# Two-layer graph attention on one core: the last step's order with v last, and the first step's norm and products in another order

## The chip, the cores and the metric

The kernel runs on one core of a Trainium2 chip. The metric is the device time of one execution in microseconds (us). Before the change the median of three runs is 3420.51 us (3420.47 to 3423.61). The core's engines are TensorE (PE in the profile; its weight loads are PEld), VectorE (DVE), ScalarE (ACT), GpSimd (POOL) and SyncE (SP), which issues nearly all DMAs. Each engine carries out its own queue in order.

## The reference

`x` holds 64 graphs of 256 nodes with 512 features, `adj` a 256x256 mask for each graph. Two layers follow each other, each with a residual:

```python
h = jnp.maximum(_layernorm(x, axis=-1), 0.0)
x = x + L0(h, adj)      # q, k, v = h@Wq, h@Wk, h@Wv   4 heads of 64; softmax(where(adj, q k^T / 8, -max)) v; @Wo + bo
h = jnp.maximum(_layernorm(x, axis=-1), 0.0)
x = x + L1(h, adj)      # layernorm(h)*gamma+beta, then w_qkv; 8 heads of 64; mask adj | eye; softmax; @w_out.T + b_out
```

All of it is float32. A row of `adj` without a neighbour gives an even average in layer 0; in layer 1 the diagonal is always allowed.

## The kernel before

`fast_path` takes the 64 graphs in 32 steps of two graphs (`G = 2`, `NSTEP = 32`). The 512 nodes of a step are four tiles of 128 rows (`NT`). Layer 1 of a step runs beside layer 0 of the next ones. A second function, `general_path`, is run only if a flag made from `extremes` says that a softmax sum was out of bounds; here it isn't run.

Steps are numbered from 0 to 31. A call such as `scores` (31, 1, 3) is step 31, layer 1, head pair 3; layer 1 has four pairs (0 to 3), layer 0 two. For each step:

- `load_h`, `load_x` bring in `x` twice, for the norm (`h`) and for the residual (`xt`). `norm0` takes the statistics of a tile on DVE (`moments`, L566 and L567), an inverse root is raised on POOL (`row_scales`, L574), and ACT scales the rows (L582; L598 in step 0).
- `transpose_h` (L641; `first_transposes`, L658, in step 0) turns `h` on TensorE; ACT evacuates it into `hT`.
- A product of two large matrices is computed as seven products of half-size blocks instead of eight (`PRODUCT` names the two blocks of each). Products 1 and 2 need raw blocks only; the others need sums of blocks: the weights' are made once (`weight_sum`, L405), those of `hT` and `oT1` in each step on POOL by `act_sums0` (block 3) and `act_sums1` (blocks 4, 5, 6), L408 to L413. `project_qk` (L741) and `project_v1` (L782) and `combine1` (L807) are such sets of seven; `project_v0` (L768) and `combine0` (L793) are plain. `evacuate` and `accumulate` add each product into its place on DVE or copy it on ACT. Some products share a PSUM bank (`SHARED`): product 2 goes on in the bank of product 1 once ACT has copied that.
- `scores` (L839) gives q k^T of a head pair into four PSUM banks, `mask_scores` adds the mask on DVE (L852), `exponentials` on ACT (L857) gives `p`, `key_halves` adds the two halves of the keys, on POOL (L865; on DVE for pairs 1 and 3 of step 31), for the sums.
- `weigh` multiplies `p` with v (L874), copies the result to `oT` on ACT (L888), and sums `pd` over the keys with a matrix of ones (L894). `invert` takes the reciprocals on DVE (L904), notes an extreme (L905), and copies them to the 64 partitions of each head with eight small DMAs (L916, into `invb`). `normalise` multiplies `oT` by `invb` (L921), on POOL, or on DVE for pairs 1 and 3 of the last step.
- `combine1` closes the step; `second_bias` (L621) has added the output's bias to `xt` on POOL beforehand, and `store` or, in step 31, `store_block` writes the result.

In steps 0 and 1 `neighbours` (L506), `neighbours_turn` (L524, L527) and `adjacency_turn` (L540) prepare the row `ne`, which tells whether a node has a neighbour, and the turned mask; `masks` makes `n0` and `n1`. `weight_block` (L463, L468) turns the four 512x512 blocks of w_qkv and w_out (block 3) on TensorE.

The order is written out by hand. A call `at(period, place, fn, ...)` puts a function at a place; the list is sorted by place, and the functions are called in that order. One unit of place is about one set of seven products, and a period is 6.13. TensorE, DVE, ACT and POOL take their instructions in this order:

```python
ctx.enter_context(tc.manual_schedule(engines={mybir.EngineType.PE, mybir.EngineType.DVE,
                                              mybir.EngineType.Activation, mybir.EngineType.Pool}))
```

SP is not in that list: the place of its transfers among each other comes from the framework's planner. `visit(period, w, prev, cur)` places one head pair's `weigh`, `invert` and `normalise` and another pair's `scores`, `mask_scores`, `exponentials` and `key_halves`. The PSUM banks of the products turn in a ring of four, `ps_sc` has four more for scores and weighings. Several SBUF buffers exist once: `inv`, `invb`, `pd`, `u`, `h`, `hT`.

## Time and profile before

| | us |
|---|---|
| runs, median of three | 3420.51 |
| profiled execution | 3424.45 |
| its span, first to last instruction | 3422.7 |
| TensorE busy in the span | 3383.6 |
| POOL busy | 1990.5 |
| DVE busy | 1907.1 |
| ACT busy | 1248.1 |
| one period in the middle, 210.57 to 315.26 (the first product set of layer 1, by the chain) | 104.69 |

The mean granted TensorE clock is 0.997. In a timeline row the first number is the start in us from the span's start, the second the length, then engine, line, operation, what is written and read; "x8" is the number of instructions merged in the row, and the bracket is the idle time of the engine before it and what ended that. In a row of the windows stand for each engine its busy us (and instructions) within the stretch, then the granted clock as a share of full speed, the busy share of the DMA engines and GB/s.

### The profile page before, as it was taken

The page shows a single profiled execution, that of the slowest core. Times are in us where ns is not written, and L with a number is a line of the kernel's source. Part 1 is how long each engine was busy: PE and PEld are TensorE (multiplying, and loading weights), DVE is VectorE, ACT ScalarE, POOL GpSimd, SP SyncE. Part 2 cuts the span into 40 slices and gives each one's busy share as a digit, 9 for nine tenths or more (in the row PEclk, how much of TensorE's full clock was granted, in tenths as well). Part 3 has the DMA queues.
Part 4 walks back from the last instruction along what each step waited for, and adds up shares of the span by engine and source line. Part 5 has one row for each costly group of instructions (what it writes and reads, how often), then busy time and mean ns, then how long its engine had stood idle before and what let it go on. Part 6 is the DMA issues. An engine that isn't in the chain of part 4 may idle for free.

```text
span 3422.7 us, 59225 instructions
## 1 busy us (share of the span) xinstructions
PE 3383.6 (99%) x22602; PEld 2627.8 (77%) x22602; DVE 1907.1 (56%) x3392; ACT 1248.1 (36%) x2201; POOL 1990.5 (58%) x1854
## 2 busy tenths in 40 slices
PE   8999999999999999999999999999999999999998
PEld 6787777777777877777777778777777777787766
DVE  5655556555565555565555655555655556555554
ACT  3433443333333333433333333334333433333421
POOL 5655665556655556655566555566555665555641
PEclk9999999999999999999999999999999999999999
DMA  3112111211111111111111112111111111211011
GB/s 128 42 58 56 38 50 46 57 57 54 32 47 56 58 56 34 53 47 56 57 54 32 47 57 58 57 30 52 52 56 56 55 32 46 57 58 50 22 42 38
DMA packets 167697, 173.89 MB, mean 51 GB/s; under 512 B 59624, under 2 KB 112368, under 8 KB 167408
## 3 DMA queue, kind: packets, MB, share of 16 engines
q1 hardware_dynamic: 167200, 169.91, 16.9%
q8 instruction: 180, 2.95, 0.4%
q14 instruction: 109, 0.89, 0.1%
q10 hardware_dynamic: 208, 0.14, 0.0%
HBM read 85.99 MB, written 33.62 MB: 35 GB/s over the span
## 4 chain that ended last, share of the span: by engine, by line
PE 97%; DVE 1%; ACT 0%; SPq 0%; DMA 0%; issue 0%; POOL 0%; ACTq 0%; DVEq 0%; POOLq 0%
PE mm L741 34%; PE mm L782 11%; PE mm L807 11%; PE sc L839 11%; PE sc L874 10%; PE mm L768 6%; PE mm L793 6%; PE mm L641 3%; PE mm L894 2%; PE mm L540 0%; SPq L916 0%; DVE inv L904 0%; ACT h L582 0%; DMA invb<-inv 0%; DVE bs L566 0%
## 5 line engine op out<-in xcount | busy, mean ns | idle before, releaser
L865 POOL TENSOR_TENSOR pd<-p 128x512 f32<-128x512 f32 x380 | 478.4, 1274 | 664.1 <-ACT p L857 564.0
L741 PE MATMUL mm<-hT,wqkv 128*128 128x256 f32 x3584 | 797.2, 381 | 0.0
L741 PEld LDWEIGHTS mm<-hT,wqkv 128*128 128x128 f32 x3584 | 673.3, 190 | 108.8 <-issue 21.1
L857 ACT ACTIVATE p<-p 128x512 f32<-128x512 f32 x768 | 459.2, 629 | 463.0 <-DVE p L852 462.0
L904 DVE RECIPROCAL inv<-mm 128x128 f32<-128x128 f32 x384 | 339.7, 926 | 374.4 <-PE mm L894 343.7
L852 DVE TENSOR_TENSOR p<-sc,n 128x512 f32<-128x512 f32 x768 | 481.1, 682 | 5.6 <-PE sc L839 5.6
L888 ACT COPY oT<-sc 128x512 f32<-128x512 f32 x192 | 112.3, 585 | 1007.9 <-PE sc L874 981.7
L741 PE MATMUL mm<-hT,wqk 128*128 128x256 f32 x1792 | 406.0, 384 | 2.5 <-DVE wqk L405 1.9
L807 PE MATMUL mm<-wo,oT 128*128 128x256 f32 x1792 | 396.1, 381 | 5.1 <-DVE oT L921 3.5
L921 POOL TENSOR_TENSOR oT<-oT,invb 128x512 f32<-128x512 f32 x190 | 241.9, 1273 | 270.7 <-DMA invb<-inv 244.5
L741 PEld LDWEIGHTS mm<-hT,wqk 128*128 128x128 f32 x1792 | 340.0, 191 | 72.3 <-DVE inv L904 9.9
L782 PE MATMUL mm<-wqkv,hT 128*128 128x256 f32 x1792 | 395.3, 381 | 0.0
L839 PE MATMUL sc<-qk 64*128 64x256 f32 x3072 | 384.2, 389 | 1.4 <-ACT oT L888 1.4
L874 PE MATMUL sc<-p,v 128*32 128x256 f32 x6144 | 377.6, 384 | 5.6 <-ACT p L857 5.6
L782 PEld LDWEIGHTS mm<-wqkv,hT 128*128 128x128 f32 x1792 | 337.8, 190 | 55.3 <-issue 10.6
L807 PEld LDWEIGHTS mm<-wo,oT 128*128 128x128 f32 x1792 | 339.8, 191 | 52.4 <-DVE oT L921 4.3
L839 PEld LDWEIGHTS sc<-qk 64*128 64x128 f32 x3072 | 281.2, 186 | 106.0 <-issue 77.8
L874 PEld LDWEIGHTS sc<-p,v 128*32 128x32 f32 x6144 | 181.3, 110 | 173.0 <-issue 64.6
L709 POOL TENSOR_TENSOR xt<-xt,u 128x512 f32<-128x512 f32 x93 | 118.0, 1269 | 246.4 <-DVE xt L702 183.9
L582 ACT ACTIVATE h<-h,mr,r 128x512 f32<-128x512 f32 x252 | 197.5, 809 | 118.9 <-POOL mr L578 118.8
L793 PE MATMUL mm<-wo,oT 128*128 128x512 f32 x512 | 230.3, 593 | 0.0
L768 PE MATMUL mm<-wv,hT 128*128 128x256 f32 x1024 | 230.2, 382 | 0.0
(112 smaller groups left out, 3664.0 us busy)
## 6 DMA issues: line engine op xcount, KB each, us to landing
invb<-inv SPq DMA_DIRECT2D x1532, 32.0 KB, 1.8
xt<-in_x_dram SPq DMA_DIRECT2D x32, 1024.0 KB, 5.5
h<-in_x_dram SPq DMA_DIRECT2D x31, 1024.0 KB, 5.4
out_dram<-xt SPq DMA_DIRECT2D x31, 1024.0 KB, 4.5
ne<-row SPq DMA_DIRECT2D x30, 256.0 KB, 4.1
ad<-in_adj_dram SPq DMA_DIRECT2D x32, 128.0 KB, 12.5
wr<-in_L_gnn_w_qkv_dram SPq DMA_DIRECT2D x3, 1024.0 KB
h<-in_x_dram SPq DMA_DIRECT2D x4, 256.0 KB, 3.8
```

The source lines that it names most:

```text
L741: nc.tensor.matmul(bank[:, k, :], w[:, wa, c, k, a * P:(a + 1) * P], st["hT"][:, ba, c, :], start=first and (k, c) == (0, 0), stop=(k, c) ...
L768: nc.tensor.matmul(bank, st["hT"][:, b0 + t // NIC * step, c % HC, i:i + P], wv0[:, c, :], start=(c == 0), stop=(c == NC - 1),)
L782: nc.tensor.matmul(bank[:, t, :], st["hT"][:, ba, c, t * P:(t + 1) * P], wqkv1[:, wa, c, 2, :], start=first and (t, c) == (0, 0), stop=(t, ...
L793: nc.tensor.matmul(bank, st["oT0"][:, pr, t // NIC, t % NIC * P:(t % NIC + 1) * P], wo0[:, pr, :], start=(pr == 0), stop=(pr == PR0 - 1),)
L807: nc.tensor.matmul(bank[:, t, :], st["oT1"][:, ba, c, t * P:(t + 1) * P], wo1[:, wa, c, :], start=first and (t, c) == (0, 0), stop=(t, c) ...
L839: nc.tensor.matmul(sc[g][e][:, kc, :], qk[rows, 1, k0:k0 + P], qk[rows, 0, g * N:(g + 1) * N], start=True, stop=True,)
L852: nc.vector.tensor_tensor(p[e][:, g], sc[e], neg[:, :, g, :], ALU.add)
L857: nc.scalar.activation(p[e][:, g], p[e][:, g], AF.Exp, scale=SCALE)
L865: engine_of(s, lyr, pr).tensor_tensor(pd[:, e], p[e][:, :, 0, :], p[e][:, :, 1, :], ALU.add)
L874: nc.tensor.matmul(po[r0:r0 + 32, g, :], st[f"v{lyr}"][:, g * NIC + kc, pr * P + r0:pr * P + r0 + 32], p[r0 // DH][:, g, kc, :], start=(kc ...
L904: nc.vector.reciprocal(inv[:, i * P:(i + 1) * P], sums[:, i * P:(i + 1) * P])
L921: engine_of(s, lyr, pr).tensor_tensor(dst, dst, invb, ALU.mult)
```

## The change

**The last step (31).**
- Layer 1's order was q and k of pairs 0 and 2, v, q and k of pairs 1 and 3, with each pair's weighing as soon as it was ready, and the combine at the end. It is now q and k (0, 2); step 30's combine; q and k (1, 3); v. The four pairs' scores, key sums and inverses lie between these products. The four weighings follow v directly, then the combine.
- `weigh` is split: `weigh_out` (as before, with the copy on ACT) and `key_sums`. In the last step `weigh_last` multiplies the PSUM result by `invb` on DVE as it writes `oT`, so ACT's copy and `normalise` are gone there.
- The transposes of step 31 come ahead of step 30's combine; its second statistics are taken close together, its scales two rows at a time; half of its `hT` is evacuated by DVE; `act_sums` of `hT` move to DVE. `second_bias` comes later.
- Step 30's pairs 1 and 3 are visited at other places, its combine comes later. Four pairs' `p`, `pd`, `inv` and `invb` live at once, so some use buffers of other tiles that are free by then (`h`, `oT0`, `v0`, `wo0`, `wv0`, `n0`, `ne`, `ab`, `u`). Half the copies of the inverses of pair 1 go out on ACT's queue, as those of pair 3 did already.

**The first steps.**
- `norm0` of step 0 is split: the statistics of the next tile go ahead of `first_scale` of the one before.
- Step 0's first set goes 1, 2, 6, 5, 7, 3, 4 instead of 1, 6, 5, 2, 7, 3, 4, with `adjacency_turn` before product 2.
- `neighbours_rows` (the four DVE instructions of L524) is taken out of `neighbours_turn` and placed earlier in step 1, ahead of step 0's first key sums.
- The four blocks of w_out are turned between the products of step 0's first set of layer 1, not before its scores. Step 0's `second_bias` comes later, its scales of layer 1 two rows at a time and earlier; odd chunks of its `hT` in layer 1 are evacuated by DVE.

The middle steps' calls stay as they are. The core of the diff:

```diff
+    def neighbours_rows(s):
+        rows = S[s]["rows"] = sm.tile([P, NT, P], BF, name="rows", tag="u", bufs=1)
+        for t in range(NT):
+            nc.vector.tensor_scalar(rows[:, t, :], onesb, S[s]["any"][:, t:t + 1], None, op0=ALU.mult)
...
+    def first_scale(t):
+        st = S[0]
+        r, mr = st["r"][:, t:t + 1], st["mr"][:, t:t + 1]
+        nc.vector.tensor_scalar(mr, st["mean"][:, t, 0:1], r, -1.0, op0=ALU.mult, op1=ALU.mult)
+        nc.scalar.activation(st["h"][:, t, :], st["h"][:, t, :], AF.Identity, bias=mr, scale=r)
...
+        part = 2 if s in (0, NSTEP - 1) else NT
+        if t % part == part - 1:
+            rows = slice(t + 1 - part, t + 1)
...
+            row_scales(s, ve, rows)
...
+        elif s in (0, NSTEP - 1) and c % 2:
+            nc.vector.tensor_scalar(
+                dst, ph, gb[:, 0, c:c + 1], gb[:, 1, c:c + 1], op0=ALU.mult, op1=ALU.add
+            )
...
+        last = (s, lyr) == (NSTEP - 1, 1)
+        if last and pr == 1:
+            both = act.tile([P, 2, G, NIC, N], FP, name="p", tag="h")
+            p = [both[:, e] for e in range(2)]
+        elif last and pr == 3:
+            p = [act.tile([P, G, NIC, N], FP, name="p", tag=tag) for tag in ("oT0", "v0")]
...
+    def weigh_last(pr):
+
+        po, dst = weigh(NSTEP - 1, 1, pr, pr == 0)
+        nc.vector.tensor_tensor(dst, po, S[NSTEP - 1]["invb", 1, pr], ALU.mult)
...
-                    queue = nc.scalar if d0 % DH and (s, lyr, pr) == (NSTEP - 1, 1, 3) else nc.sync
+                    queue = nc.scalar if d0 % DH and last and pr in (1, 3) else nc.sync
...
+    LAST_QK = 4.0
+    for s in range(-1, NSTEP - 1):
+        p, tail = s, s == NSTEP - 2
...
+        visit(p, 3.685 if tail else AT_Q0 + 2 / 7, (s, 1, 1, False), (s, 1, 3), 0.03 if tail else 0.0)
         if s >= 0:
-            visit(p, AT_V0, (s, 1, 3, False), (s + 2, 0, 0))
+            visit(p, LAST_QK + 3 / 7 if tail else AT_V0, (s, 1, 3, False), (s + 2, 0, 0))
+
+    none = (NSTEP,)
+    p = NSTEP - 2
+    for w, i, pr in (
+        (LAST_QK + 1, 5 / 7, 0), (LAST_QK + 1 + 3 / 7, 5 / 7, 2), (LAST_QK + 3, 5 / 7, 1), (LAST_QK + 3 + 2 / 7, 4 / 7, 3)
+    ):
+        visit(p, w, none, (NSTEP - 1, 1, pr))
+        at(p, w + i - 0.0005, key_sums, NSTEP - 1, 1, pr)
+        at(p, w + i, invert, NSTEP - 1, 1, pr)
+    for i, pr in enumerate((0, 1, 2, 3)):
+        at(p, LAST_QK + 4 + 0.01 * i, weigh_last, pr)
...
+            if s == 0:
+                at(p, 0.95 + 0.4 * t, first_scale, t)
...
-            at(p, (3.857, 3.59)[s], neighbours_turn, s)
+            at(p, (3.72, 2.72)[s], neighbours_rows, s)
+            at(p, (3.855, 3.59)[s], neighbours_turn, s)
...
+        order = SET if s else (1, 2, 6, 5, 7, 3, 4)
...
-            at(p, (3.55, 3.7, 4.05, 4.2)[t] - back, norm1_rest, s, t)
-            at(p, 3.62 + 0.08 * t, second_bias, s, t)
-            at(p, 4.5 + 0.1 * t - back, scale_row, s, t)
+            at(p, AT_C0 + 0.3 + 0.14 * t - back if (s, t) != (NSTEP - 1, 3) else 3.69, norm1, s, t)
+            at(p, ((3.55, 3.7, 4.05, 4.2) if s < NSTEP - 1 else (3.55, 3.6, 3.7, 3.705))[t] - back, norm1_rest, s, t)
+            at(p, 3.62 + 0.08 * t if 0 < s < NSTEP - 1 else 6.5 + 0.1 * t, second_bias, s, t)
+            at(p, 4.5 + 0.1 * t if 0 < s < NSTEP - 1 else (4.25 if s == 0 else 3.71) + 0.003 * t, scale_row, s, t)
...
+            at(p, (AT_H1 if s < NSTEP - 1 else 3.8) + 0.0001 * c, transpose_h, s, 1, c)
+        at(p, AT_C1 + 0.15 if s < NSTEP - 1 else 3.95, lambda s=s: act_sums0(S[s]["hT"], nc.gpsimd if s < NSTEP - 1 else nc.vector))
...
+            at_set(p, AT_C1 if not last else LAST_QK + 1, SETC, combine1, s)
...
+            at_set(p, LAST_QK, SET, project_qk, s, 1, 0)
+            at_set(p, LAST_QK + 2, SET, project_qk, s, 1, 1)
+            at_set(p, LAST_QK + 3, SET, project_v1, s)
+            at(p, LAST_QK + 4.015, lambda s=s: act_sums0(S[s]["oT1"], nc.vector))
+            at(p, LAST_QK + 4.035, lambda s=s: act_sums1(S[s]["oT1"], nc.vector))
+            at_set(p, LAST_QK + 4.1, (1, 5, 2, 3, 6, 7, 4), combine1, s)
...
-        place = 3.3 - 3.93 + (1 + i) / 7 - 0.0005 if i < 4 else 0.2 + 0.07 * i if i < 8 else 1.62 + 0.075 * (i - 8)
+        place = 3.3 - 3.93 + (1 + i) / 7 - 0.0005 if i < 4 else 0.2 + 0.07 * i if i < 8 else 1.62 + 0.1 * (i - 8) if i < 12 else 6.2 + 1 / 7 * (i - 12)
```

## The prediction

> **What bounds the kernel now.** I read the page, then the windows, then the timeline at both ends.
>
> The page's engine line and TensorE's 40 slices:
>
> ```profile
> PE 3383.6 (99%) x22602; PEld 2627.8 (77%) x22602; DVE 1907.1 (56%) x3392; ACT 1248.1 (36%) x2201; POOL 1990.5 (58%) x1854
> PE   8999999999999999999999999999999999999998
> ```
>
> TensorE is idle for 3422.7 - 3383.6 = 39.1 us. The windows (columns: PE, PEld, DVE, ACT, POOL busy, granted clock, DMA share, GB/s) put all of it in the first 100 us and the last 125; between, a period repeats every 104.69 us with no gap:
>
> ```profile
> 0.00:25.00 25.00, 14.32 (x45) 10.34 (x46) 15.46 (x34) 7.22 (x9) 10.42 (x17) 1.00 0.94 310
> 3300.00:3325.00 25.00, 18.11 (x126) 10.39 (x125) 14.74 (x31) 13.11 (x22) 14.49 (x16) 0.87 0.11 27
> 3375.00:3400.00 25.00, 17.91 (x174) 10.31 (x172) 14.54 (x24) 6.64 (x11) 1.46 (x2) 1.00 0.09 22
> 3400.00:3423.00 23.00, 14.49 (x55) 11.15 (x55) 12.29 (x22) 0.58 (x1) 0.00 (x0) 0.88 0.20 60
> ```
>
> The timeline names the waits. Start: products wait for DVE's weight sums (L405); later four weights stand behind `rows` (L524), slow while POOL adds (L493); then transposes (L641) wait for rows of `h`.
>
> ```profile
> 13.22 3.78 PE L741 MATMUL mm<-hT,wqk 128*128 128x256 f32 x8
> 13.99 6.46 DVE L405 TENSOR_TENSOR wqk<-wqk 128x512 f32<-128x512 f32 x4
> 18.93 3.75 PE L741 MATMUL mm<-hT,wqk 128*128 128x256 f32 x8 [1.93 <-DVE wqk L405]
> 54.24 4.44 DVE L524 TENSOR_SCALAR rows<-onesb,any_of 128x128 bf16<-128x128 bf16 x4
> 54.93 4.93 POOL L493 TENSOR_TENSOR xt<-xt,bo_b 128x512 f32<-128x512 f32 x4
> 58.74 0.29 PE L527 MATMUL mm<-identb,rows 128*128 128x128 bf16 x1 [0.99 <-DVE rows L524]
> 97.10 3.03 PE L641 MATMUL mm<-ident,h 128*128 128x128 f32 x13 [1.42 <-ACT h L582]
> ```
>
> End: the last step's transposes wait, and its final weighings and combine wait for exponentials and inverses.
>
> ```profile
> 3317.40 0.33 PE L641 MATMUL mm<-ident,h 128*128 128x128 f32 x1 [2.41 <-ACT h L582]
> 3322.82 13.48 PE L807 MATMUL mm<-wo,oT 128*128 128x256 f32 x56
> 3394.67 1.44 PE L874 MATMUL sc<-p,v 128*32 128x256 f32 x14 [2.14 <-ACT p L857]
> 3400.17 4.97 PE L807 MATMUL mm<-wo,oT 128*128 128x256 f32 x14 [2.78 <-DVE oT L921]
> 3407.51 6.74 PE L807 MATMUL mm<-wo,oT 128*128 128x256 f32 x30 [0.74 <-DVE oT L921]
> 3415.03 1.99 PE L807 MATMUL mm<-wo,oT 128*128 128x256 f32 x8 [0.78 <-DVE xt L698]
> ```
>
> A wait costs twice: the clock sinks (0.50 from 3319 to 3325), and 56 matmuls then take 13.48 us instead of 12.09.
>
> **The end, costed.** Durations start to start, warm: weighing 1.75, key sums 0.55, scores 1.93, 16 transposes 1.93 (0.121 each, row at 43.58), a set of seven products 12.28 (1.76 each), a combine 12.09. From 3302.99, the weighing of (30,1,1), both kernels have six weighings, six sums, five scores, the transposes, three sets and two combines: 10.5 + 3.3 + 9.65 + 1.93 + 36.84 + 24.18 = 86.4. Without a wait TensorE would end at 3389.4; its last matmul ends at 3417.0. Lost: 27.6.
>
> After, I place each engine's queue in its new order.
> - DVE: `norm1` and `norm1_rest` of the four tiles run together, ahead of `invert` (30,1,1). Statistics cost 0.87 a tile; the last `h` leaves ACT at 3307.75 as now, so DVE ends them at 3308.75 (now 3313.2).
> - POOL: `second_bias` (4 x 1.27) has left the stretch for the last step's second product set, where POOL has only key halves and step 30's last sums (6 us of work in 12). The scales come two rows at a time, 2.14 us from statistics to ACT now; a power of four columns takes 1.01, of one 0.56, so 0.71 for two and 1.84 in all. Rows 2 and 3 reach ACT at 3310.7.
> - ACT: two rows at about 0.75 end at 3312.2, then exponentials to 3313.4, then half the evacuations (0.78).
> - TensorE has nothing from 3307.2 to 3312.2 but three transposes, so it goes cold as at 3318. The remaining 13 take 3.04 cold, to 3315.3; product 1 follows, half cold, to about 3318.5. Product 6 needs a block sum: DVE evacuates until 3316.05, masks (2 x 0.62), then makes the sums, now DVE's: 0.65 each, b4 at 3318.65.
> - These sums meet POOL's two `key_halves`. Where that happens now (four weight sums in 3.88 at 69.33, with one POOL multiply) one sum took 1.64 instead of 0.69: I take b4 and product 6 at 3320.0. Without a wait product 6 would start at 3310.9. Lost: 9.1.
>
> The Trainium skill (SBUF — State Buffer, "Who interferes with whom") calls the shared port pair an exclusive lock for a whole instruction. By it, POOL first both times would give b4 at 3321.35, and the sum would be 1.35 worse.
>
> - `invert` (30,1,3): its reciprocals end at 3327.6; eight copies on SP (0.59 each) and the landing take 6.57, as from 64.72 to 71.29. `normalise` (1.27) and one POOL sum end at 3336.8, and product 5 of step 30's combine waits 0.25.
> - `inv` has one buffer, so the inverse of pair 2 waits 2.6 us on DVE; products 6, 5, 2 (5.3 us) cover it, and without them it costs 2.6.
> - v last: pair 3's inverse is ready at 3381 and copied over two queues by 3385 (4.17, as at 3402.6 to 3406.76), while TensorE weighs until 3387. The multiplies (0.69) take over `normalise`, and the ACT copies (0.58) vanish. The block sums (0.6 each) run beside products 1 and 5, so the 2.78 and 0.74 waits go. The 0.78 ahead of product 4 stays, and the stores' tail with it.
>
> The new places of `p`, `pd` and `invb` cost nothing: their old owners (`h` after the transposes, `oT0`, `v0`, `wo0`, `wv0`, `n0`, `ne`, `ab`) are last read before 3316, the first new writer comes after 3345; were one late, a scores row (1.93) would wait. Scores laid between products find their four banks free, since the masks before them (2.5 us) run beside at least two products.
>
> Lost after: 9.1 + 0.25 + 0.8 = 10.1. The end gains 17.5. Bounds: 18.9 (no meeting with POOL) to 11 (2.6 of DVE's wait, 2 on the copies, 1.8 from the flag's code, which made DVE wait that long at 3405).
>
> **The start, costed.**
> - Norm: DVE goes on to the next tile instead of waiting 0.66 to 0.76 for POOL's power. The fourth tile of `h` lands only at 7.1 (2.2 + 4.9), and both neighbour maxima (2 x 0.64) now stand ahead of the last scale: its ACT row starts at 9.9, not 11.19. Gain 1.3; bounds 0 (later landings) and 1.6.
> - Order 1, 2: product 2 needs no sum. Product 1 starts at 11.9, then `adjacency_turn` and product 2 fill what was the 1.93 wait and more. The weight sums end at 19.1, `rows` (0.73) at 19.9, the turn (0.4) at 20.3, product 6 (1.76) at 22.1: four products remain. Now that point is 25.97. Further gain 2.6; bounds 1.5 and 3.
> - `rows` of step 1 move to where DVE idles 7.05 us (40.5 to 47.58). Beside `key_halves` they may take 4.44 again, still hidden. TensorE's turn shrinks from 2.75 to 0.4 and the next weighing stays warm (1.75, not 3.3). Gain 3.9; bounds 2 and 3.9.
> - The w_out blocks (16 transposes, 1.9) leave the place before the scores for step 0's first set: no gain in itself, and about 0.5 of bank waits there (0.32 and 0.56 at the earlier blocks). `load_x` (1) waits for them on SP; `xt` is wanted 40 us later. Two rows' scales are ready 3 us earlier, odd evacuations move to DVE. Transposes end at 95.5 or, cold, 97, against 100.1. Net gain 2.6 warm, 0.6 cold: I take 1.6, -1 and 2.6 as bounds.
>
> The row says cold may come early: at 59 the clock read 0.50 after about 2.5 us of near idleness, and here it is 2.2. The Trainium skill (TensorE: Matmul & The Clock Gate, Part 1) puts the gate at an idle window of about 3.4 us. By that rule it stays warm: 1 us more gain.
>
> Start: 1.3 + 2.6 + 3.9 + 1.6 = 9.4; bounds 2.5 and 11.
>
> **Sum.** 17.5 + 9.4 = 26.9. The profiled execution took 3424.45 (span 3422.7 and 1.75 around it): 3397.55. It stands 3.94 above the runs' median 3420.51, so on that scale 3393.6; I say 3394.
>
> **Rivals.**
> 1. *The start's gain is eaten* (landings, cold clock, bank waits; for it: DMA share 0.94 there; against: step 1's `h` landed at 22.4, four us before use). 3420.5 - 17.5 - 2.5 = 3400.5.
> 2. *The end turns its wait rather than losing it*: TensorE still idles before the transposes, and DVE's in-order inverses hold evacuations back. For: 9.1 of 27.6 stays. 11 + 4 = 15 gained: 3405.5; if waits on copies fall on TensorE three times (6.57 each), 7 us of both ends' gain are left, the edge of no change.
> 3. *Slower*: SP is not among the four engines whose order is fixed, so its transfers may be planned anew in every period. If the copies of the inverses came late behind loads, `normalise` and then TensorE would wait. It decides from 26.9 / 31 = 0.87 us a period; 1.2 a period gives 3431. Against: the middle periods' calls are the same in the same order, and `normalise` waits now without stopping TensorE (244.5 us in 49 waits).
>
> **Numbers.** Forecast 60%, within 3387 to 3399. Rival 1 16%, rival 2 14% (a third of it no change), rival 3 5%, the rest unforeseen. 3387 to 3409 should hold 8 in 10. No change is within 0.2% (6.8 us), about what a measurement can tell: faster 0.88, same 0.05, slower 0.07.
>
> **What would show it.** TensorE busy near 98 to 99% with some 20 us idle; one gap of 5 us before the L641 transposes of the last step and none before its weighings; combine matmuls in one run with one wait of 0.8; `rows` before 45 us; product 6 after product 2. Wrong if the middle period leaves 104.69, if the inverses hold DVE for more than 5 us, or if the flag's code or a copy stops the last weighings.

## The result and the profile after

The kernel after takes 3401.54 us (median of five executions, 3401.24 to 3403.0), the kernel before beside it 3421.27 us (five, 3420.47 to 3423.75). The ratio is 0.9941, with a 95% interval of 0.9927 to 0.9956: 19.7 us faster. The prediction was 3394, in a range from 3387 to 3409. The profiled execution of after took 3401.54 us, which happens to be its median; its span is 3399.3. Profiled execution against profiled execution the gain is 3424.45 - 3401.54 = 22.9 us, where the prediction's sum was 26.9.

The line numbers of after differ: L755 is `project_qk`, L796 `project_v1`, L821 `combine1`, L853 `scores`, L896 `weigh`, L930 `key_sums`, L651 the transposes of `h`, L530 the turn of `rows`, L887 `key_halves`.

The page of after, its engine line and TensorE's 40 slices:

```profile
PE 3373.3 (99%) x22602; PEld 2621.7 (77%) x22602; DVE 1919.5 (56%) x3402; ACT 1243.2 (37%) x2193; POOL 1991.2 (59%) x1858
...
PE   8999999999999999999999999999999999999999
```

TensorE is idle for 3399.3 - 3373.3 = 26.0 us instead of 39.1, and the last slice now reads 9. The windows of after (PE, PEld, DVE, ACT, POOL busy, granted clock, DMA share, GB/s):

```profile
0.00:25.00 25.00, 15.95 (x65) 12.01 (x66) 16.73 (x36) 8.39 (x11) 15.08 (x21) 1.00 0.98 310
...
3300.00:3325.00 25.00, 20.87 (x118) 16.32 (x120) 17.73 (x25) 8.12 (x13) 6.22 (x7) 0.86 0.09 22
...
3350.00:3375.00 25.00, 25.00 (x172) 18.95 (x174) 17.94 (x30) 6.27 (x11) 0.00 (x0) 1.00 0.10 25
3375.00:3400.00 25.00, 17.55 (x149) 13.25 (x141) 11.78 (x20) 0.59 (x1) 0.00 (x0) 0.96 0.17 53
```

From 3350 to 3375 TensorE is busy without a gap; before, its last 48 us held seven waits. Of the 26.0 us that are left, 9.1 lie in the first 25 us, 4.1 in the 25 us around the last step's transposes, where the clock is at 0.86, and 6.1 behind the last matmul; most of the rest lies between 50 and 125 us. The timeline of after on TensorE, at the start:

```profile
11.62 3.78 PE L755 MATMUL mm<-hT,wqk 128*128 128x256 f32 x8
...
16.08 1.99 PE L755 MATMUL mm<-hT,wqk 128*128 128x256 f32 x8
...
19.87 0.71 PE L530 MATMUL mm<-identb,rows 128*128 128x128 bf16 x4 [1.80 <-DVE rows L524]
20.45 8.87 PE L755 MATMUL mm<-hT,wqk 128*128 128x256 f32 x40
...
52.44 0.39 PE L530 MATMUL mm<-identb,rows 128*128 128x128 bf16 x4
...
86.26 1.64 PE L651 MATMUL mm<-ident,h 128*128 128x128 f32 x13 [0.38 <-ACT h L585]
```

Product 1 starts at 11.62 (13.22 before), product 2 follows without a weight sum, the wait has moved to the turn of `rows` (1.80), step 1's turn has none (0.39 in one row), and step 0's transposes run warm. At the end:

```profile
3303.14 0.48 PE L651 MATMUL mm<-ident,h 128*128 128x128 f32 x1 [1.69 <-ACT h L585]
3303.84 3.03 PE L651 MATMUL mm<-ident,h 128*128 128x128 f32 x13 [0.23 <-ACT h L585]
3306.68 3.25 PE L755 MATMUL mm<-hT,wqkv 128*128 128x256 f32 x8
...
3311.34 3.69 PE L755 MATMUL mm<-hT,wqkv 128*128 128x256 f32 x16 [1.42 <-DVE hT L411]
...
3328.61 3.72 PE L821 MATMUL mm<-wo,oT 128*128 128x256 f32 x16 [0.32 <-POOL oT L408]
...
3372.78 7.11 PE L896 MATMUL sc<-p,v 128*32 128x256 f32 x128
3379.82 10.63 PE L821 MATMUL mm<-wo,oT 128*128 128x256 f32 x48
...
3391.23 1.99 PE L821 MATMUL mm<-wo,oT 128*128 128x256 f32 x8 [0.68 <-DVE xt L712]
```

The four last weighings are one row of 128 matmuls, the six first products of the last combine one row of 48, and the only wait behind them is the 0.68 ahead of the last product. What idle time the end still has before its last matmul is in front: rows of `h`, cold transposes, and block sum b4 of `hT` (L411) ahead of product 6.

To tell start and end apart, I cut every execution at one instruction, the weighing of (30, 1, 0), which both parts of the change leave alone. "Start" is its time in the profiled execution, "end" the stretch from it to the end of the last matmul. The middle is the same in both kernels (104.69 us from period to period: layer 1's first product sets of after, by the chain, at 202.45, 307.13, 411.82). One traced execution stands behind each start and end, the median is that of all executions.

| kernel | median | start | end |
|---|---|---|---|
| before | 3421.27 | 3275.20 | 141.82 |
| after | 3401.54 | 3267.08 | 126.14 |
| e1_end_only | 3406.40 | 3274.15 | 125.85 |
| e2_rows_back | 3405.9 | 3270.37 | 126.15 |
| e3_order_back | 3401.66 | 3268.23 | 126.14 |
| e4_wout_back | 3401.39 | 3266.97 | 127.50 |
| e5_sums_first | 3400.87 | 3269.17 | 124.61 |
| e6_warm | 3399.78 | 3267.27 | 124.75 |
| e7_fill | 3396.78 | 3269.56 | 119.74 |
| e8_split | 3401.45 | 3267.12 | 126.14 |
| e9_fill_wout | 3395.37 | 3267.01 | 119.74 |
| e10_fill_warm | 3394.91 | 3267.16 | 119.73 |
| e11_head_warm | 3401.21 | 3266.78 | 127.83 |
| e12_v_middle | 3408.64 | 3269.35 | 132.93 |

After gains 8.1 us at the start and 15.7 at the end, and loses 0.4 behind the last matmul (5.68 to 6.08): 23.4, the difference of the spans. The median of e2_rows_back leaves out a fifth execution of 3906.66 us, whose mean granted clock was 0.85.

### The profile page after: what moved, and what is told of

Its sections match the earlier page's. It is cut to its first block, busy times and chain, and to the rows that moved or that the text cites. A ratio compares the mean times of both kernels' runs of the same rounds, so it can differ in the third digit from the quotient of the medians.

```text
span 3399.3 us, 59198 instructions
## 1 busy us (share of the span) xinstructions
PE 3373.3 (99%) x22602; PEld 2621.7 (77%) x22602; DVE 1919.5 (56%) x3402; ACT 1243.2 (37%) x2193; POOL 1991.2 (59%) x1858
## 4 chain that ended last, share of the span: by engine, by line
PE 97%; DVE 1%; ACT 0%; issue 0%; DMA 0%; POOL 0%; SPq 0%; DVEq 0%; POOLq 0%
PE mm L755 34%; PE mm L796 12%; PE mm L821 11%; PE sc L853 11%; PE sc L896 10%; PE mm L782 6%; PE mm L807 6%; PE mm L651 3%; PE mm L930 2%; PE mm L543 0%; DVE bs L569 0%; ACT h L585 0%; DVE wqk L405 0%; DVE wqkv L405 0%; DVE inv L940 0%
## 5 line engine op out<-in xcount | busy, mean ns | idle before, releaser
L887 POOL TENSOR_TENSOR pd<-p 128x512 f32<-128x512 f32 x378 | 477.2, 1278 | 631.6 <-ACT p L882 523.3
L755 PE MATMUL mm<-hT,wqkv 128*128 128x256 f32 x3584 | 800.0, 382 | 2.6 <-DVE hT L411 1.4
L755 PEld LDWEIGHTS mm<-hT,wqkv 128*128 128x128 f32 x3584 | 673.8, 190 | 112.6 <-issue 23.1
L755 PE MATMUL mm<-hT,wqk 128*128 128x256 f32 x1792 | 403.4, 382 | 0.7 <-ACT wqkv L468 0.6
L796 PE MATMUL mm<-wqkv,hT 128*128 128x256 f32 x1792 | 396.1, 381 | 0.0
L821 PE MATMUL mm<-wo,oT 128*128 128x256 f32 x1792 | 393.3, 379 | 1.0 <-DVE xt L712 0.7
L755 PEld LDWEIGHTS mm<-hT,wqk 128*128 128x128 f32 x1792 | 338.4, 191 | 69.5 <-DVE inv L940 9.9
L853 PE MATMUL sc<-qk 64*128 64x256 f32 x3072 | 384.1, 389 | 0.0
L796 PEld LDWEIGHTS mm<-wqkv,hT 128*128 128x128 f32 x1792 | 337.6, 190 | 56.3 <-issue 11.4
L821 PEld LDWEIGHTS mm<-wo,oT 128*128 128x128 f32 x1792 | 337.6, 190 | 47.7 <-issue 1.5
L896 PE MATMUL sc<-p,v 128*32 128x256 f32 x6144 | 370.7, 382 | 0.0
L853 PEld LDWEIGHTS sc<-qk 64*128 64x128 f32 x3072 | 281.2, 186 | 104.2 <-issue 77.6
L896 PEld LDWEIGHTS sc<-p,v 128*32 128x32 f32 x6144 | 180.3, 109 | 162.0 <-issue 61.5
```

Source lines behind the costliest of these rows:

```text
L755: nc.tensor.matmul(bank[:, k, :], w[:, wa, c, k, a * P:(a + 1) * P], st["hT"][:, ba, c, :], start=first and (k, c) == (0, 0), stop=(k, c) ...
L796: nc.tensor.matmul(bank[:, t, :], st["hT"][:, ba, c, t * P:(t + 1) * P], wqkv1[:, wa, c, 2, :], start=first and (t, c) == (0, 0), stop=(t, ...
L821: nc.tensor.matmul(bank[:, t, :], st["oT1"][:, ba, c, t * P:(t + 1) * P], wo1[:, wa, c, :], start=first and (t, c) == (0, 0), stop=(t, c) ...
L853: nc.tensor.matmul(sc[g][e][:, kc, :], qk[rows, 1, k0:k0 + P], qk[rows, 0, g * N:(g + 1) * N], start=True, stop=True,)
L887: eng.tensor_tensor(pd[:, e], p[e][:, :, 0, :], p[e][:, :, 1, :], ALU.add)
L896: nc.tensor.matmul(po[r0:r0 + 32, g, :], st[f"v{lyr}"][:, g * NIC + kc, pr * P + r0:pr * P + r0 + 32], p[r0 // DH][:, g, kc, :], start=(kc ...
```

## The experiments

**Is it two parts that add up?** e1_end_only keeps the end of after and undoes the part at the first steps. Here and below "..." stands for lines of a diff or a view that are left out.

```diff
-        part = 2 if s in (0, NSTEP - 1) else NT
+        part = 2 if s == NSTEP - 1 else NT
...
-            at(p, (3.72, 2.72)[s], neighbours_rows, s)
-            at(p, (3.855, 3.59)[s], neighbours_turn, s)
+            at(p, (3.8565, 3.589)[s], neighbours_rows, s)
+            at(p, (3.857, 3.59)[s], neighbours_turn, s)
...
-        order = SET if s else (1, 2, 6, 5, 7, 3, 4)
+        order = SET
...
```

> The kernel after, with the part at the first steps undone: step 0's norm in one piece, its first set as 1, 6, 5, 2, 7, 3, 4, the rows, the turns, the scales of step 0, the odd evacuations of step 0 and the w_out blocks where they stood before. Theory (two parts that do not touch each other): the first parts' 8.1 us go and nothing else, so the weighing of (30,1,1) starts at 3303.0 instead of 3294.9, the stretch from there to the end of the last matmul stays 98.35 us, and the time is 3401.5 + 8.1 = 3409.6. Rival (the start's gain lets transfers of the middle run earlier, or the end lives on it): the period leaves 104.69 or the last stretch differs from 98.35 by more than 1 us.

Measured: 3406.40 us (four executions, 3404.24 to 3408.97), ratio to before 0.995 (0.9934 to 0.9967). The end is 125.85, within 0.3 of after, and from the last four products of step 0's first set to the weighing of (30, 1, 0) it takes 3249.3 us, in before 3249.2: the two parts do not touch each other. But the time is 3.2 below the expected 3409.6. By the medians the end is worth 14.9 us (3421.27 - 3406.40) and the first steps 4.9 (3406.40 - 3401.54), where the starts of the profiled executions differ by 8.1. What the old first steps cost varies: the four executions of this run spread over 4.7 us, the five of after over 1.8. The start in the profiled execution, too, is 1.05 us earlier than in before, though the code up to there is in the old order. The timeline of e1_end_only shows where, in the second product, at the row that before had as 18.93 with 3.75:

```profile
18.95 2.55 PE L755 MATMUL mm<-hT,wqk 128*128 128x256 f32 x8 [1.98 <-DVE wqk L405]
```

The same eight matmuls after nearly the same wait (1.93 there) took 2.55 instead of 3.75. What such a stretch costs differs from execution to execution, and the next runs show it again.

**The rows of step 1.** e2_rows_back fills `rows` right before the turn again.

```diff
-            at(p, (3.72, 2.72)[s], neighbours_rows, s)
+            at(p, (3.72, 3.589)[s], neighbours_rows, s)
```

> The kernel after, with the four scalings that fill rows for step 1 back right before the turn that reads them. Theory (the four weights stood behind DVE beside POOL's additions): the wait ahead of the turn near 55 us comes back with the cold clock behind it, 3.9 us from there to the end: 3405.4. Rival (the gap was covered by something later in the first steps, the transposes' wait for rows of h): the turn waits, but the first product of (0,1,0) stays within 1 us of 93.35 and the time within 1 us of 3401.5.

Measured: 3404.4 to 3407.1 us, ratio 0.9952 (0.9937 to 0.9968). The start is 3.3 later, of which 0.74 had arisen already by the turn of step 0 (20.61 instead of 19.87: the third row tile of `h` landed late). So 2.6 belong to the rows in this execution. The timeline of e2_rows_back on TensorE:

```profile
54.91 0.23 PE L530 MATMUL mm<-identb,rows 128*128 128x128 bf16 x1 [0.99 <-DVE rows L524]
56.13 0.23 PE L530 MATMUL mm<-identb,rows 128*128 128x128 bf16 x1 [0.99 <-DVE rows L524]
56.29 1.93 PE L896 MATMUL sc<-p,v 128*32 128x256 f32 x32
```

and that of before, at the same weighing (its granted clock was 0.50 from 59 to 62):

```profile
58.96 3.48 PE L874 MATMUL sc<-p,v 128*32 128x256 f32 x32
```

The two waits of 0.99 are back to the hundredth, but the weighing behind them stayed at full clock here and did not in before. The rows are worth 2.6 us when the clock holds and about 1.55 more (3.48 - 1.93) when it falls; the predicted 3.9 was the second case. The profiled execution is the shortest of the four; their median, 3405.9, is 4.4 above after and 0.5 above the expected 3405.4. The rival, that something later covers it, falls.

**The order of the first set.** e3_order_back puts products and turns of step 0 back, and keeps the norm.

```diff
-            at(p, (3.72, 2.72)[s], neighbours_rows, s)
-            at(p, (3.855, 3.59)[s], neighbours_turn, s)
+            at(p, (3.8565, 2.72)[s], neighbours_rows, s)
+            at(p, (3.857, 3.59)[s], neighbours_turn, s)
-        at(p, (3.7125, 3.583)[s] if s < 2 else 2.2, adjacency_turn, s)
+        at(p, (3.716, 3.583)[s] if s < 2 else 2.2, adjacency_turn, s)
-        order = SET if s else (1, 2, 6, 5, 7, 3, 4)
+        order = SET
```

> The kernel after, with step 0's first set in the order 1, 6, 5, 2, 7, 3, 4 and the turns of the adjacency and of the neighbour rows of step 0 at their old places; the norm tile by tile stays. Theory: the second product again waits for a weight sum, and the four-products-left point, 22.2 after, comes 2.2 us later (of the 3.8 that this point gained, 1.6 stands already at product 1): 3403.7. Rival (the loads set that point, DMA share 0.98 in the first 25 us): the wait moves to another product and the time stays within 0.7 us of 3401.5.

Measured: 3401.66 us (3400.09 to 3402.23), start 1.15 later in the profiled execution. By the medians this is the rival's case, 0.1 from after; the profiled start lies between the two expectations. The timeline of e3_order_back:

```profile
17.44 3.65 PE L755 MATMUL mm<-hT,wqk 128*128 128x256 f32 x8 [2.54 <-DVE wqk L405]
20.88 0.66 PE L543 MATMUL mm<-identb,adb 128*128 128x128 bf16 x8
21.38 1.95 PE L755 MATMUL mm<-hT,wqk 128*128 128x256 f32 x8
```

and that of before behind the row at 18.93 with 3.75:

```profile
22.47 1.06 PE L540 MATMUL mm<-identb,adb 128*128 128x128 bf16 x8
23.33 2.58 PE L741 MATMUL mm<-hT,wqk 128*128 128x256 f32 x8
```

The wait for the weight sum is 2.54, and in after 1.80 of it stand at the turn of `rows` instead: the new order moves most of the wait rather than losing it. The point with four products left is at 23.38 here, 22.2 in after and 25.97 in before, where the norm is undone as well. So of these 3.8 the order is worth 1.2 instead of the predicted 2.6. Of the other 2.6, 1.5 stand already at product 1 (11.74 instead of 13.22), which is the norm (predicted 1.3). The last 1.1 belong to no part of the change: here the two products and the turn between take 3.65, 0.66 and 1.95, in before 3.75, 1.06 and 2.58, and e1_end_only, with norm and order both old, has its four products left at 24.88, as much earlier.

**The w_out blocks.** e4_wout_back puts the last eight blocks back ahead of the scores.

```diff
-        place = 3.3 - 3.93 + (1 + i) / 7 - 0.0005 if i < 4 else 0.2 + 0.07 * i if i < 8 else 1.62 + 0.1 * (i - 8) if i < 12 else 6.2 + 1 / 7 * (i - 12)
+        place = 3.3 - 3.93 + (1 + i) / 7 - 0.0005 if i < 4 else 0.2 + 0.07 * i if i < 8 else 1.62 + 0.075 * (i - 8)
```

> The kernel after, with the last eight w_out blocks back ahead of the scores of step 0's first set. Theory A (the 2.45 us of waits among the moved blocks, 1.19 for ACT's wo and 0.82 for DVE's qk sum, come from their new place): the set of (0,1,0) to its v1 falls from 20.92 to about 16.6, its start moves from 93.35 to about 95.2, net 2.45 faster: 3399.1. Theory B (DVE's weight sums there are slow for second_bias on POOL, 5.41 at 97.02, whatever the blocks do): the wait for DVE's qk stays and at most 1.2 is gained: 3400.3. Rival (the transposes of step 0 wait longer once the blocks no longer stand behind them, and the clock falls): 0 to 1 slower.

Measured: 3401.39 us (3400.09 to 3402.58). The timeline of after at the moved blocks:

```profile
99.14 1.99 PE L755 MATMUL mm<-hT,wqkv 128*128 128x256 f32 x8 [1.19 <-ACT wo L468]
...
101.95 0.66 PE L463 MATMUL mm<-ident,wr 128*128 128x128 f32 x4 [0.82 <-DVE qk L691]
```

and that of e4_wout_back at its last product and at the last step's product 6:

```profile
107.97 1.96 PE L755 MATMUL mm<-hT,wqkv 128*128 128x256 f32 x8 [1.42 <-DVE qk L695]
...
3310.91 5.38 PE L755 MATMUL mm<-hT,wqkv 128*128 128x256 f32 x16 [2.13 <-DVE hT L411]
```

The waits for the blocks go, and one for DVE (1.42) comes; the weight sums (L405) stand there beside POOL's second bias, whose four additions took 6.30 us in this run, but no run tells the two apart. The start is 0.11 earlier, after a turn that was 0.36 later (20.23): the old place is worth 0.5 us, theory B with less than it allowed. Moving the blocks was a small loss inside the change. The end of this run is 1.4 longer although nothing was changed there: the clock read 0.50 from 3312 to 3314 and products 6 and 5 took 5.38 instead of 3.69. The profiled execution (3402.56) is one of two long ones; the two short ones, 3400.09 and 3400.22, lie where theory B put the time, and have no trace.

**The wait for b4.** e5_sums_first puts the last step's block sums ahead of the masks of (30, 1, 3) on DVE.

```diff
-        at(p, AT_C1 + 0.15 if s < NSTEP - 1 else 3.95, lambda s=s: act_sums0(S[s]["hT"], nc.gpsimd if s < NSTEP - 1 else nc.vector))
-        at(p, AT_C1 + 0.5 if s < NSTEP - 1 else 3.96, lambda s=s: act_sums1(S[s]["hT"], nc.gpsimd if s < NSTEP - 1 else nc.vector))
+        at(p, AT_C1 + 0.15 if s < NSTEP - 1 else 3.81, lambda s=s: act_sums0(S[s]["hT"], nc.gpsimd if s < NSTEP - 1 else nc.vector))
+        at(p, AT_C1 + 0.5 if s < NSTEP - 1 else 3.815, lambda s=s: act_sums1(S[s]["hT"], nc.gpsimd if s < NSTEP - 1 else nc.vector))
```

> The kernel after, with the block sums of hT of the last step put ahead of the masks of (30,1,3) on DVE. Theory (the sixth product of the last step's first set stands behind masks, 1.28, and behind a sum that took 1.57 beside POOL's key halves where another took 0.68): b4 comes about 2.1 us sooner, the wait of 1.42 goes, 3400.1. Rival (the next evacuations or the later weighing take the wait over, since masks and exponentials of (30,1,3) now come 2 us later): the wait of 1.42 goes, a new one of the same size comes before the key sums of (30,1,3), and the time stays within 0.5 of 3401.5.

Measured: 3400.87 us (3400.47 to 3401.87); the end is 1.53 shorter, as the theory has it, and no new wait comes before the key sums. The median is only 0.7 lower. In the profiled execution, the longest of the four, the start is 2.1 longer (below); the others have no trace. The sums on DVE and the additions on POOL in the timeline of after:

```profile
3309.63 1.57 DVE L411 TENSOR_TENSOR hT<-hT 128x512 f32<-128x512 f32 x1
3311.12 1.75 DVE L412 TENSOR_TENSOR hT<-hT 128x512 f32<-128x512 f32 x1
...
3309.07 3.25 POOL L887 TENSOR_TENSOR pd<-p 128x512 f32<-128x512 f32 x2 [6.83 <-ACT p L882]
```

and in e5_sums_first, with product 1 on TensorE:

```profile
3310.52 0.69 DVE L411 TENSOR_TENSOR hT<-hT 128x512 f32<-128x512 f32 x1
3311.13 0.68 DVE L412 TENSOR_TENSOR hT<-hT 128x512 f32<-128x512 f32 x1
...
3313.75 2.51 POOL L887 TENSOR_TENSOR pd<-p 128x512 f32<-128x512 f32 x2 [9.43 <-ACT p L882]
...
3308.76 6.83 PE L755 MATMUL mm<-hT,wqkv 128*128 128x256 f32 x24
```

Apart from POOL a sum takes 0.69 and POOL's two additions 2.51; together they take 1.57 to 1.75 and 3.25. A sum beside POOL lasts about its own time and most of one addition (1.25), so the two seem to take turns, which fits the exclusive lock of the Trainium skill (SBUF — State Buffer, "Who interferes with whom") for two inputs in SBUF. With the sums first, products 1, 6 and 5 are one row of 24 without a wait.

**The clock before the transposes.** e6_warm adds work there.

```diff
+    def keep_warm():
+        bank = mm_tile([P, 4 * P])
+        for r in range(24):
+            nc.tensor.transpose(bank[:, r % 4 * P:(r % 4 + 1) * P], ident, ident)
+
+    at(NSTEP - 2, 3.7, keep_warm)
```

> The kernel after, with 24 transposes of the identity added between the scores of (30,1,3) and the last step's transposes of h; nobody reads what they write. Theory 1 (the cold clock there, 0.50 from 3304 to 3308, is a cost of its own): the 13 transposes after the last row of h take 1.6 instead of 3.03 and the first product 1.76 each instead of a cold start; the sixth product still waits for b4, which comes sooner by up to 1 us since its evacuations do: about 1 us faster, 3400.5. Theory 2 (the rows of h, then DVE and ACT, set the sixth product): the transposes are shorter, the wait before the sixth product grows by as much, 3401.5 within 0.4.

Measured: 3399.78 us (3399.55 to 3401.62); the end is 1.39 shorter. The timeline of e6_warm:

```profile
3299.81 2.84 PE L1019 MATMUL mm<-ident 128*128 128x128 f32 x24
...
3304.03 1.64 PE L651 MATMUL mm<-ident,h 128*128 128x128 f32 x13 [0.38 <-ACT h L585]
...
3310.14 3.69 PE L755 MATMUL mm<-hT,wqkv 128*128 128x256 f32 x16 [2.34 <-DVE hT L411]
```

The transposes take 1.64 instead of 3.03. The wait for b4 grows from 1.42 to 2.34, so part of the shorter time becomes wait as theory 2 says, but the evacuations and with them b4 come 1.4 sooner, counted from the weighing of (30, 1, 0) (42.87 instead of 44.26): theory 1, and a little more than its size. It is the transposes' part of the cold clock that counts. In six traces (after, e1_end_only, e2_rows_back, e3_order_back, e8_split, e11_head_warm) product 6 starts 44.26 us after that weighing, whether product 1 ahead of it takes 1.99 us or 3.25.

**Other work in the gap.** e7_fill moves the last step's first combine and second norm ahead of step 30's second product set. With them go the places of step 30's last two pairs, of the inverses and of the block sums, so it tests the new arrangement as a whole.

```diff
-    LAST_QK = 4.0
+    LAST_QK = 3.05
...
-            at_dense(p, AT_C0 + 0.01 + 0.14 * t - back, 0.14, combine0, s, t)
+            if s < NSTEP - 1:
+                at_dense(p, AT_C0 + 0.01 + 0.14 * t - back, 0.14, combine0, s, t)
+            else:
+                at_dense(p, 1.9998 + 0.00003 * t, (0.041, 0.051, 0.071, 0.091)[t], combine0, s, t)
...
-            at(p, (AT_H1 if s < NSTEP - 1 else 3.8) + 0.0001 * c, transpose_h, s, 1, c)
+            at(p, (AT_H1 if s < NSTEP - 1 else 3.0001) + 0.0001 * c, transpose_h, s, 1, c)
...
```

> The kernel after, with the last step's first combine and its second norm ahead of step 30's second product set, so that this set and the last step's products lie between the rows of h and their transposes. Theory (of the 12.0 us that TensorE loses from the weighing of (30,1,1) to its last matmul, some 8.6 are the wait before the transposes, the cold clock and the wait for b4, and all of it needs only other work in between): 6 to 8 us faster, 3394 to 3396, and the clock stays at 1.00 there. Rival (the wait is turned: DVE, with the norm beside the second set's evacuations and masks, holds banks or exponentials back): 0 to 3 us faster, with new waits of TensorE for p or for a bank.

Measured: 3396.78 us (3396.44 to 3397.17), ratio 0.9928 (0.991 to 0.9946). The end is 6.4 shorter, within the expected 6 to 8, with the clock at 1.00; the time is 0.8 above the expected 3394 to 3396. The end in the timeline of e7_fill, three rows:

```profile
3297.16 1.97 PE L651 MATMUL mm<-ident,h 128*128 128x128 f32 x16
3298.96 2.18 PE L755 MATMUL mm<-hT,wqkv 128*128 128x256 f32 x8
3301.79 3.69 PE L755 MATMUL mm<-hT,wqkv 128*128 128x256 f32 x16 [0.65 <-DVE hT L411]
```

All 16 transposes run as one row with no wait, and of the waits up to product 6 only 0.65 is left. But the time fell by 4.8, not 6.4: in the profiled execution the start, where nothing was changed, was 2.5 longer. The start in the same timeline:

```profile
11.77 1.99 PE L755 MATMUL mm<-hT,wqk 128*128 128x256 f32 x8
...
20.02 0.77 PE L530 MATMUL mm<-identb,rows 128*128 128x128 bf16 x4 [3.58 <-DVE rows L524]
20.60 11.23 PE L755 MATMUL mm<-hT,wqk 128*128 128x256 f32 x40
```

Product 1 took 1.99 here and 3.78 in after. `rows` come at 20.0 either way, so the wait is 3.58 instead of 1.80, and the 40 matmuls behind it take 11.23 instead of 8.87, the clock at 0.50 from 19 to 25. A first product that was 1.8 us quicker was followed by 2.4 us more behind the wait.

**The folded multiply.** e8_split makes each of the four last multiplies in two steps again.

```diff
-        nc.vector.tensor_tensor(dst, po, S[NSTEP - 1]["invb", 1, pr], ALU.mult)
+        nc.scalar.copy(dst, po)
+        nc.vector.tensor_tensor(dst, dst, S[NSTEP - 1]["invb", 1, pr], ALU.mult)
```

> The kernel after, with each of the four multiplies of the last weighings by their inverses made as before in two steps, a copy on ACT and then a multiply on DVE. Theory (products 1 and 5 of the last combine, 2 x 1.7 us, cover the evacuations and the sums): no wait appears, 3401.5 within 0.5. Rival (folding the copy into the multiply was worth its 0.58 for the last pair): 0.6 to 1.2 slower, with a wait before the last combine's first or second product.

Measured: 3401.45 us (3401.35 to 3403.16), end 126.14, the same as after. The fold is worth nothing in time: with the four copies back, no wait appears ahead of the last combine's products, since the copies, multiplies and sums end beside products 1 and 5. The last combine in the timeline of e8_split:

```profile
3379.86 10.63 PE L821 MATMUL mm<-wo,oT 128*128 128x256 f32 x48
```

**Both changes to after that helped.** e9_fill_wout is e7_fill with the w_out blocks at their old place (the two diffs above together).

> The kernel with the last step's first combine moved forward (e7_fill) and also the w_out blocks back ahead of the scores of step 0's first set (e4_wout_back). Theory (the two are apart by 3200 us and add up; in e4_wout_back the weighing of (30,1,1) came 0.11 us earlier after a start that was 0.37 us later, so the blocks' old place is worth 0.48): 0.5 faster than e7_fill's 3396.8, 3396.3. Rival (the blocks' place is worth nothing): 3396.8 within 0.3.

Measured: 3395.37 us (3394.57 to 3396.72), ratio 0.9924 (0.991 to 0.9937). The end is e7_fill's to the hundredth. The profiled start is 0.07 shorter than after's with a turn that was 0.42 later, so 0.5 again; the median is 0.9 below the expected 3396.3. That may be the start's clock, which held in this profiled execution (wait 1.73, 40 matmuls in 8.87); the other four have no trace.

**The clock at the start.** e10_fill_warm is e7_fill with 14 transposes ahead of step 0's turn; e11_head_warm is after with the same.

```diff
+    def keep_warm():
+        bank = mm_tile([P, 4 * P])
+        for r in range(14):
+            nc.tensor.transpose(bank[:, r % 4 * P:(r % 4 + 1) * P], ident, ident)
+
+    at(-2, 3.8549, keep_warm)
```

> The kernel e7_fill with 14 transposes of the identity added before step 0's turn of the neighbour rows, where TensorE waits for rows; nobody reads what they write. Theory (e7_fill lost some 2.4 us of its gain at the start: its first product ran at full clock, the wait for rows therefore was 3.58 instead of 1.80, the clock fell to 0.50 and the 40 matmuls behind it took 11.23 instead of 8.87): the 40 matmuls take 8.9, 3394.5. Rival (the drop has other causes than the idle time, or the added work comes in the way of the turn): 3396.8 within 0.5 or more.

> The kernel after with the same 14 transposes before step 0's turn, nothing else. Theory (single executions of the kernel after that are about 2 us longer, 3403.0 beside 3401.3, are those in which the clock falls at that wait): the short executions stay at 3401.3 within 0.4 and the long ones vanish. Rival (they have another cause): executions at 3403 remain.

Measured, e10_fill_warm: 3394.91 us (3394.62 to 3394.97), ratio 0.9921 (0.9908 to 0.9935). Five executions lie within 0.35 us, 1.9 under e7_fill and 0.4 above the theory, and the timeline shows the start that theory wanted:

```profile
17.57 1.69 PE L1008 MATMUL mm<-ident 128*128 128x128 f32 x14
...
19.98 0.71 PE L530 MATMUL mm<-identb,rows 128*128 128x128 bf16 x4 [0.72 <-DVE rows L524]
20.55 8.87 PE L755 MATMUL mm<-hT,wqk 128*128 128x256 f32 x40
```

Product 1 took 3.34 us in this execution, as in e12_v_middle below, where without the added transposes the 40 matmuls took 10.56.

e11_head_warm: 3401.21 us (3400.77 to 3402.41). Its start is as quick as after's, yet a longer execution remained, the profiled one, and its timeline names another place:

```profile
3311.04 5.38 PE L755 MATMUL mm<-hT,wqkv 128*128 128x256 f32 x16 [1.87 <-DVE hT L411]
```

This is e4_wout_back's case: at the last step's product 6 the clock falls a second time in some executions, for 1.7 us. The theory on the start holds for e7_fill and e10_fill_warm; in e11_head_warm the rival is right as well, there is a second place. Which of the two made after's longest execution, 3403.0, stays open, since that one has no trace. e10_fill_warm, in which the gap at the end is filled too, has neither.

**V last by itself.** e12_v_middle makes v the middle set of the last step again.

```diff
-            at_set(p, LAST_QK + 2, SET, project_qk, s, 1, 1)
-            at_set(p, LAST_QK + 3, SET, project_v1, s)
+            at_set(p, LAST_QK + 3, SET, project_qk, s, 1, 1)
+            at_set(p, LAST_QK + 2, SET, project_v1, s)
...
-    for i, pr in enumerate((0, 1, 2, 3)):
-        at(p, LAST_QK + 4 + 0.01 * i, weigh_last, pr)
+    for place, pr in ((4.15, 0), (4.83, 1), (4.16, 2), (4.9, 3)):
+        at(p, LAST_QK + place, weigh_last, pr)
...
```

> The kernel after, with v of the last step as the middle set again and the second product set last, so that the scores of pairs 1 and 3, their exponentials, key halves, sums and inverses come behind the last set; the weighings of pairs 0 and 2 lie between them. All else as after. Theory (v last is what hides the exponentials and the last inverse): the last set ends at about 3367.7 on the scale of after; scores, masks (4 x 0.62), exponentials and key halves of pair 3 end near 3380, its sums and reciprocals near 3383, the copies (4.2) near 3387.3, the multiply near 3388; products 1 and 5 of the last combine run ahead, product 2 starts near 3388.3 instead of 3383.3: 5 us slower, 3406.5, and up to 9 if products 1 and 5 wait too. Rival (the end's gain came from the norm and the rows of h alone, and any order with both inverses ahead of the combine hides them): 3401.5 within 1.

Measured: 3408.64 us (3408.13 to 3410.25), ratio 0.9962 (0.9949 to 0.9976): 7.1 slower than after, its end 6.8 longer (the start has one of the falls of the clock, with 10.56 us for its 40 matmuls). The timeline of e12_v_middle:

```profile
3381.91 1.25 PE L930 MATMUL mm<-pd,ones 128*32 128x256 f32 x5 [4.51 <-DVE pd L887]
...
3383.19 5.76 PE L896 MATMUL sc<-p,v 128*32 128x256 f32 x63
```

The wait is 4.51 for pair 3's key halves, which on DVE stand behind masks and pair 1's reciprocals, and the weighings behind it are slow: the clock reads 0.50 from 3381 to 3387, and 63 matmuls take 5.76 us where 64 took 3.66 at 3371. So against this one arrangement with v in the middle, v last is worth 6.8 us of end, some 2 of them through the clock; another order on DVE might lose less and was not tried. By subtraction 8.9 of the end's 15.7 us are left for everything else in the last step.

## Why the prediction was right, and where it was not

The direction and the two ends were right; 3401.54 lies inside 3387 to 3409, but outside the 3387 to 3399 that the forecast's 60% stood for. It is 7.9 us above the sum's 3393.6 and 1.0 from rival 1's 3400.5, so the wide range held by the rivals' room in it. On the scale of the profiled executions the end gave 15.3 instead of 17.5 (with the 0.4 behind the last matmul), the start 8.1 instead of 9.4, and the time around the span grew by 0.5 (1.75 to 2.24): 4.0 together. The other 3.9 came from the last step, the scale. By the medians (e1_end_only) the end gave 14.9 and the start only 4.9, so the start was the term that was sized worse.

- **The scale.** "It stands 3.94 above the runs' median 3420.51, so on that scale 3393.6" took for granted that after's profiled execution would stand as high above its median. It stands on it. What the runs show is that the profiled execution of before held slow stretches in its start that do not come every time (3.48 or 1.93 for one weighing, 3.75 or 2.55 for one product). The prediction counted the removal of these stretches in full and then took the 3.94 off as well; e1_end_only, with a start worth 4.9 by the medians and 8.1 by the traces, fits that. That the clock accounts for all of the 3.94 is argued, not shown: before has one trace, and the mean clocks speak neither for nor against it. Its four longest other executions (3424.94 to 3425.26) read 0.997, most of those near 3421 read 0.996, and the column reads 1.00 even while the product takes 3.75.
- **The end, up to product 6: 9.1 lost.** Product 6 starts at 3311.34, that is 3311.34 + 8.12 = 3319.46 on the scale of before, predicted 3320.0; the loss is 8.6. The meeting with POOL that was costed by the row at 69.33 is there (1.57; the case with POOL first both times, 3321.35, did not come), and e5_sums_first confirms cause and size. Of the signs, the gap ahead of the last transposes is 3.0 us in four pieces rather than 5 in one, and TensorE idles 26.0 us rather than some 20.
- **The end, behind it.** Product 5 of step 30's combine waits 0.32 (0.25), the last product 0.68 (0.8), the last weighings and products 1 and 5 not at all, and pair 2's inverse waits on DVE for 4.20 rather than 2.6, still covered. These make 9.6. But the stretch from the weighing of (30, 1, 1) to the last matmul went from 114.03 to 98.35, 15.7 less, so 11.9 of the 27.6 are still lost. The term that was missed is the price of breaking sets up: with scores and sums inside, the last v set takes 12.91 without them (3356.84 to 3372.78, less 1.93 and two sums of 0.55) against 12.28 whole, step 30's combine 12.86 against 12.09. All such pieces together come to about 1.7 us over seven places where a set is broken, near 0.2 for each. The prediction had set them at nothing. Some 0.6 of the 11.9 stay unplaced.
- **Norm and order, 1.3 + 2.6.** Together 3.8 in the traces (predicted 3.9), but that is luck: e3_order_back puts the norm at 1.5 and the order at 1.2, and 1.1 are slow stretches of the profiled execution of before, which e1_end_only lacks with the same old code. The step that failed is "`adjacency_turn` and product 2 fill what was the 1.93 wait and more": 1.80 of the wait is now ahead of the turn of `rows`.
- **Rows of step 1, 3.9.** The trace of after has 4.0 less (7.76 at the next set, 3.78 before it), but e2_rows_back shows 2.6 for the waits in an execution in which the clock held, and 4.4 by the medians.
- **w_out and scales, 1.6.** Measured 0.6 (8.12 in all, 7.52 at the v0 before). The transposes stayed warm, which was the 2.6 case (the waits ahead of them came to 1.07 us in three pieces, not 2.2, so this does not test the 3.4 us window); "about 0.5 of bank waits" was 1.19 and 0.82 in two waits, and undoing the blocks alone gains 0.5 in the trace.
- **Rivals.** The first (the start's gain eaten to 2.5) is wrong by the traces, where 8.1 of 9.4 are there, and half right by the medians, where 4.9 are. What ate the rest, by the runs, is the order's wait, the wait for the moved blocks, and stretches of before that were slow by chance. The second (the end turns its wait) describes correctly the 8.6 us that stay ahead of product 6, but of the inverses only the 0.32 ahead of product 5 reached TensorE, and the end gained 15.3, not 11. The third (transfers planned anew) didn't happen: the period is 104.69.

## What to carry to other kernels

When the profiled execution is slower than the median, look for what in its trace is a matter of chance (here stretches at half clock behind short waits) before you take the difference off a gain that contains the same stretches. An order that hides a chain of exponentials and inverses under the last independent product set is worth what its waits cost, less (here) some 0.2 us for every place where it breaks a run of equal matmuls. A gap in front of a chain on other engines was better filled with other work of TensorE (6.4 us here) than with work that nobody reads, put there only to hold the clock (1.4).

## What the runs showed of the hardware that I had not expected

- **What TensorE gains ahead of a wait it can lose behind it.** At the start the same 40 matmuls behind the same turn of `rows` took 8.87 us after waits of 1.50 to 1.80 (after and five others), 10.56 after 2.24 and 2.40, and 11.23 after 3.58. The wait was long where product 1 had been quick (3.78, then 3.34 and 3.18, then 1.99 us). What makes product 1 take 1.99 or 3.78 in the same code isn't settled; the granted clock reads 1.00 in all of them.
- **Whether the clock falls behind a given wait differs between executions.** The same two waits of 0.99 were followed by a weighing of 3.48 (before), 3.55 (e1_end_only) and 1.93 (e2_rows_back). The Trainium skill (TensorE: Matmul & The Clock Gate, Part 1) says that the window which decides is free-running and that the count of cold matmuls varies from run to run; the runs agree with that. Its idle window of about 3.4 us is longer than the uninterrupted waits of 2.24 and 2.40 after which the clock fell here.
- **The length of the wait does not decide it either.** Ahead of the last step's product 6 the clock fell after waits of 1.87 (e11_head_warm) and 2.13 (e4_wout_back), where products 6 and 5 took 5.38, and did not after 2.34 (e6_warm), 2.51 to 2.73 (five runs) or 1.42 (after), where they took 3.69. What decides it is not settled by these runs.
